# A two-layer graph attention network on one core: layer 0's scores in four quarters of TensorE

## The chip, the core and the metric

The kernel runs on one core of one Trainium2 chip. The core has five engines that work side by side and wait for one another through semaphores: TensorE (matrix products out of SBUF into PSUM), VectorE, ScalarE, GpSimd, and SyncE, which here only issues transfers. The metric is the time of one execution on the device in microseconds; the figure quoted is the median of three runs.

## The reference

The input is x, 8 batches of 2048 nodes with 256 features, and one adjacency matrix of 2048 x 2048. Two graph layers follow, each with a residual sum and a layer norm. Layer 0 is an attention with 4 heads of 64 features, in which the softmax is taken separately in each chunk of 256 keys and the results of the 8 chunks are summed:

```python
scores = jnp.einsum('bhnd,bhjcd->bhnjc', q, kc) / jnp.sqrt(jnp.asarray(Dh, dtype=q.dtype))
scores = jnp.clip(scores, -10.0, 10.0)
mask = adj_matrix.reshape(N, Nc, CHUNK)[None, None]
scores = jnp.where(mask == 0, jnp.asarray(-10.0, scores.dtype), scores)
attn = jax.nn.softmax(scores, axis=-1)
ctx = jnp.einsum('bhnjc,bhjcd->bhnd', attn, vc)
```

Then come an output projection, a residual, a norm with scale and shift, and another residual with a norm. Layer 1 is a graph attention whose score is a sum of a source and a target term, with a leaky slope of 0.2, a mask, a softmax over all 2048 nodes, the product with the transformed features, and an ELU. All arithmetic is f32.

## The kernel before

**Tiles.** A tile has P = 128 partitions. Queries are taken CH = 512 at a time (NCH = 4 groups), heads in pairs (HP = 2), keys in chunks of 256 (NK = 8), that is KT = 2 tiles of 128 keys. One combination of a query group, a pair of heads and a chunk is a *slot*, so a batch has SLOTS = 4 x 2 x 8 = 64 slots. `qT` and `kT` hold queries and keys transposed: the partitions are the 128 features of a pair of heads (D = 64 for each head), the free axis is the nodes.

**What a slot does for layer 0.**
- `scores(s)` (line 378): for each of the two key tiles `u` it takes two PSUM banks (`ps`, one bank for each head of the pair) and issues one matmul for each head `k`. The weights (`lhsT`) are the 64 feature rows of that head for 128 keys, the moving operand is 512 queries. Head 0 lies on rows 0 to 63 of the array and head 1 on rows 64 to 127, so each matmul uses one half of the rows and all the columns (line 388).
- Line 399, on VectorE: the scores are clipped and masked out of PSUM into `pr` in SBUF, with `slab`, an 8-bit tile of upper bounds.
- `exps` (line 411), on ScalarE: the exponential of `pr`, in place.
- `product(s, k)` (line 425): for each head the probabilities are the weights, 64 queries at a time (`z` chooses a column half of the array), and the values with a column of ones are the moving operand, 65 columns. They use all 128 rows. ScalarE copies the result out (line 432), VectorE takes a reciprocal (line 440), GpSimd scales and adds (lines 447 and 449).

**PSUM.** `two_banks` (line 105) hands out two buffers of two banks in turn. So the scores of one slot fill both buffers, and the next slot's scores wait until VectorE has read them.

**Layer 1.** While layer 0 of batch b runs, layer 1 of batch b - 1 is carried along: in each slot `lower.step()` makes and uses four tiles (STEP = 4): one VectorE instruction makes `e` (line 739), and 16 matmul calls use it as weights in 64-column halves (line 761, into `pa`).

**Order.** The order on every engine is written out by hand: the kernel runs under a manual schedule, and instructions go to an engine in the order in which the code calls them. In a slot `s` of the main loop the order of TensorE's work is the scores of slot s + 1, the product of head 0 of slot s, the layer 1 step, the product of head 1 of slot s, and in some slots a projection, an output product or a transposition. In batch 0 there is no layer 1 step; masks are prepared there instead (`masks.step()`). After batch 7, layer 1 of the last batch runs alone.

Of the kernel before, what the change touches and what calls it, by code (L numbers as in the profile page):

```python
# [17 lines left out]
P = 128  # L18
# [4 lines left out]
def adj_resnorm_kernel(  # L23
# [19 lines left out]
    nc = tc.nc  # L43
    B, N, F = x.shape
    H, D = a_src.shape
# [59 lines left out]
    def two_banks(shape, name):  # L105

        turn_of[0] ^= 1
        return psA.tile(shape, F32, tag=f"psA{turn_of[0]}", name=name)
# [10 lines left out]
    qT = big.tile([P, KC, N], F32, tag="qT", name="qT")  # L119
    kT = big.tile([P, KC, N], F32, tag="kT", name="kT")  # L120
# [257 lines left out]
    def scores(s):  # L378
        q, hp, c = where[s]
        slab = slab_of.pop(s)  # L380
        cols = slice(q * CH, (q + 1) * CH)
        pss = []
        for u in range(KT):
            t = KT * c + u
            ps = two_banks([P, 2, CH], "ps")
            for k in range(2):
                rows = slice(k * D, (k + 1) * D)
                nc.tensor.matmul(  # L388
                    ps[:, k, :],
                    lhsT=kT[rows, hp, t * P : (t + 1) * P],  # L390
                    rhs=qT[rows, hp, cols],
                    start=True,
                    stop=True,
                )
            pss.append(ps)
        probs[s] = []
        for u in range(KT):
            pr = prp.tile([P, 2, CH], F32, tag="pr", name="pr")
            nc.vector.scalar_tensor_tensor(  # L399
                pr,  # L400
                pss[u],
                -CLIP,
                slab[:, u, :].unsqueeze(1).to_broadcast([P, 2, CH]),
                op0=ALU.max,
                op1=ALU.min,
            )
            probs[s].append(pr)
# [548 lines left out]
    for b in range(B):  # L956
        waug = blocks.tile([P, NT, H, D1], F32, tag="waug", name="waug")
        sd = small.tile([P, 2 * H, NT], F32, tag="sd", name="sd", bufs=1)
        if b == 0:
            for s in range(3):  # L960
                load_slab(s)
            scores(0)
            for u in range(KT):
                exps(0, u)
# [7 lines left out]
        for s in range(SLOTS):  # L972
            q, hp, c = where[s]
# [27 lines left out]
            if s + 1 < SLOTS:  # L1001
                scores(s + 1)
# [67 lines left out]
        if b + 1 < B:  # L1070
            (k0, v0, q0), (l1, t1, k1, v1, q1), (l2, t2, k2, v2, q2), (l3, t3, k3, v3, q3) = turns
            rest = [lambda: lower.rest(1)] if lower else []
            order = [begin, *rest, l1, *rest, lambda: before.values((2, 3))]
            order += [*rest, ctx, *rest, *rest, k0]
            order += [steps[0], t1, steps[1], v0, steps[2], steps[3], l2, k1, steps[4], q0]
            order += [steps[5], v1, t2, l3, steps[6], q1, steps[7], k2, steps[8], steps[9], t3, v2]
            order += [lambda: [load_slab(s) for s in range(3)], fs[0], q2, fs[1], k3, fs[2], v3]
            order += [lambda: scores(0), q3, lambda: [exps(0, u) for u in range(KT)]]
        else:

            step = lower.step
            order = [begin, lambda: before.values((2, 3)), steps[0], step, ctx, step, steps[1], step]
            order += [steps[2], step, steps[3], step, steps[4], step, steps[5], step, steps[6], step]
            order += [steps[7], step, steps[8], step, steps[9], step, fs[0], step, fs[1], step, fs[2]]
            order += [step] * 5
            assert sum(p is step for p in order) == LATE
# [64 lines left out]
```

## Time and profile before

| | |
|---|---|
| median of 3 runs | 3769.13 us (3766.95 to 3769.89) |
| the profiled execution: span from first to last instruction | 3764.9 us |
| instructions in the profile | 159631 |
| TensorE: matmul, weight loads | 3655.7 us, 2743.7 us busy |
| VectorE | 3138.5 us busy |
| ScalarE | 1979.9 us busy |
| GpSimd | 1368.3 us busy |
| runs of scores (line 388) | from 60.5 to 3490.9 us |
| mean granted TensorE clock | 0.993 |

Engines overlap, so the busy times don't add up to the span. Weight loads run beside matmuls and have a row of their own. Matmuls are pipelined and their ends are modelled, so the starts of successive records say more of the rate than their durations do. A matmul's shape is written as rows * columns of the array that hold weights, followed by the operand: `64*128 64x512` has 64 rows, 128 columns and 512 moving columns. Each f32 matmul call of the code appears as two matmul records, each with a weight load of its own: the 2048 calls of line 388 are 4096 records. The chain of waits is followed back from the last instruction to whatever released it each time. Idle time of an engine that isn't in this chain costs nothing.

### The profile page before, as it was taken

To read this page: it belongs to the slowest core of one execution; us is meant where nothing else is said; L and a number is where in the kernel's file an instruction comes from. 1 tells how busy PE (TensorE), PEld (TensorE's weight loads), DVE (VectorE), ACT (ScalarE), POOL (GpSimd) and SP (SyncE) were. 2 spreads that over 40 slices of the span, in tenths; PEclk is the share of its full clock that TensorE was granted. 3 is DMA by queue.
4 is the path that set the end of the run, shared out by engine and by line. 5 is a ranking of instruction groups with operands and counts; after the bars stand their busy time and mean duration, and the time that the engine had idled before them with its cause. 6 is when DMAs were issued, how large, how long until landed. Compare 5 with 4: busy or idle time off the path is not lost.

```text
span 3764.9 us, 159631 instructions
## 1 busy us (share of the span) xinstructions
PE 3655.7 (97%) x72100; PEld 2743.7 (73%) x72100; DVE 3138.5 (83%) x4213; ACT 1979.9 (53%) x3571; POOL 1368.3 (36%) x1202
## 2 busy tenths in 40 slices
PE   9999999999999999999999999999999999999787
PEld 5656677776777777776777767777677777776676
DVE  5877589976999689995999959998699977997899
ACT  4666455555555555554555545555555555555322
POOL 1445234333433343333443324433343333334300
PEclk9999999999999999999999999999999999999899
DMA  6653334333333343333433334333433333332344
GB/s 164 152 117 70 80 96 109 105 75 112 109 105 105 86 123 100 104 96 89 133 99 94 101 93 133 106 104 76 113 109 105 105 82 115 111 98 73 100 150 137
DMA packets 672092, 398.46 MB, mean 106 GB/s; under 512 B 427312, under 2 KB 591536, under 8 KB 671408
## 3 DMA queue, kind: packets, MB, share of 16 engines
q1 hardware_dynamic: 621408, 354.55, 35.8%
q10 hardware_dynamic: 50000, 33.70, 2.8%
q8 instruction: 564, 9.24, 1.0%
q14 instruction: 120, 0.98, 0.1%
HBM read 331.22 MB, written 56.89 MB: 103 GB/s over the span
## 4 chain that ended last, share of the span: by engine, by line
PE 84%; DVE 7%; issue 4%; ACT 3%; DMA 1%; SPq 0%; ACTq 0%; POOL 0%; DVEq 0%; POOLq 0%
PE pc L425 25%; PE ps L388 23%; PE pa L761 21%; PE pp L332 5%; PE pw L581 3%; PE po L540 3%; DVE e L739 3%; PE pv L348 2%; DVE pr L399 2%; ACT y L505 1%; ACT pr L411 1%; DVE y L560 0%; DMA xp<-in_x_dram 0%; DVE y L557 0%; ACT qT L340 0%
## 5 line engine op out<-in xcount | busy, mean ns | idle before, releaser
L399 DVE SCALAR_TENSOR_TENSOR pr<-ps,slab 128x1024 f32<-128x1024 f32 x1024 | 1193.7, 1207 | 216.4 <-PE ps L388 212.6
L425 PEld LDWEIGHTS pc<-vaug,pr 128*64 128x64 f32 x32768 | 1038.7, 138 | 404.8 <-issue 298.4
L739 DVE SCALAR_TENSOR_TENSOR e<-srow,gd,et 128x1024 f32<-128x1024 f32 x1024 | 1277.4, 1291 | 14.8 <-PE pa L761 7.6
L425 PE MATMUL pc<-vaug,pr 128*64 128x65 f32 x32768 | 1153.6, 224 | 15.1 <-ACT pr L411 9.6
L761 PE MATMUL pa<-waug,e 128*64 128x65 f32 x32768 | 1070.1, 224 | 45.6 <-DVE e L739 41.4
L761 PEld LDWEIGHTS pa<-waug,e 128*64 128x64 f32 x32768 | 1016.4, 139 | 64.0 <-DVE e L739 55.5
L411 ACT ACTIVATE pr<-pr 128x1024 f32<-128x1024 f32 x1024 | 1040.3, 1055 | 39.7 <-DVE pr L399 30.8
L388 PE MATMUL ps<-qT,kT 64*128 64x512 f32 x4096 | 1024.7, 617 | 3.6 <-DVE pr L399 2.9
L432 ACT COPY raw<-pc 128x260 f32<-128x260 f32 x1024 | 381.3, 373 | 1203.1 <-PE pc L425 1176.4
L447 POOL TENSOR_TENSOR part<-raw,rd 128x512 f32<-128x512 f32 x448 | 468.6, 1046 | 1384.5 <-DVE rd L440 1370.1
L449 POOL TENSOR_TENSOR acc<-acc,part 128x512 f32<-128x512 f32 x448 | 575.3, 1284 | 35.2
L388 PEld LDWEIGHTS ps<-qT,kT 64*128 64x128 f32 x4096 | 347.8, 186 | 321.8 <-issue 201.4
L440 DVE RECIPROCAL rd<-raw 128x8 f32<-128x8 f32 x512 | 100.8, 197 | 120.0 <-ACT raw L432 118.8
L447 POOL TENSOR_TENSOR acc<-raw,rd 128x512 f32<-128x512 f32 x64 | 66.9, 1045 | 343.5 <-DVE rd L440 343.5
L793 ACT ACTIVATE sums<-sums,dn 128x64 f32<-128x64 f32 x504 | 131.9, 337 | 12.2 <-DVE dn L787 12.2
L500 POOL TENSOR_TENSOR rs_c<-rs_c,nhalf 128x4 f32<-128x4 f32 x32 | 52.7, 1647 | 232.5 <-DVE off_c L499 232.5
L581 PE MATMUL pw<-w_sb,x1T 128*128 128x264 f32 x512 | 128.0, 398 | 4.7 <-DVE x1T L294 4.7
L540 PE MATMUL po<-wo_sb,qT 128*128 128x256 f32 x512 | 126.2, 391 | 5.7 <-DVE qT L467 2.8
L332 PE MATMUL pp<-xT,wk_sb 128*128 128x512 f32 x256 | 119.2, 609 | 7.9 <-ACT qT L340 6.6
L332 PE MATMUL pp<-xT,wq_sb 128*128 128x512 f32 x256 | 116.2, 596 | 0.0
L348 PE MATMUL pv<-wv_sb,xT 128*128 128x256 f32 x512 | 115.9, 379 | 0.0
L581 PEld LDWEIGHTS pw<-w_sb,x1T 128*128 128x128 f32 x512 | 95.0, 192 | 25.0 <-DVE x1T L294 4.9
(103 smaller groups left out, 1843.7 us busy)
## 6 DMA issues: line engine op xcount, KB each, us to landing
et<-edgeD SPq DMA_DIRECT2D x512, 256.0 KB, 3.0
slab<-clipD SPq DMA_DIRECT2D x512, 128.0 KB, 3.1
srow<-rowD SPq DMA_DIRECT2D x64, 512.0 KB, 5.1
xg<-in_x_dram SPq DMA_DIRECT2D x32, 512.0 KB, 4.9
x1D<-y ACTq DMA_DIRECT2D x32, 512.0 KB, 3.9
x1g<-x1D SPq DMA_DIRECT2D x32, 512.0 KB, 5.1
out_dram<-o SPq DMA_DIRECT2D x30, 512.0 KB, 3.4
ctxD<-acc ACTq DMA_DIRECT2D x56, 256.0 KB, 2.6
```

The lines of the kernel that those rows point to most:

```text
L332: nc.tensor.matmul(pps[c], lhsT=w[:, kc, c * P : (c + 1) * P], rhs=st["xT"][:, kc, :], start=(kc == 0), stop=(kc == KC - 1),)
L388: nc.tensor.matmul(ps[:, k, :], lhsT=kT[rows, hp, t * P : (t + 1) * P], rhs=qT[rows, hp, cols], start=True, stop=True,)
L399: nc.vector.scalar_tensor_tensor(pr, pss[u], -CLIP, slab[:, u, :].unsqueeze(1).to_broadcast([P, 2, CH]), op0=ALU.max, op1=ALU.min,)
L411: nc.scalar.activation(pr, pr, AF.Exp, scale=0.125)
L425: nc.tensor.matmul(pc[z * D : (z + 1) * D, i, :], lhsT=probs[s][u][:, k, i * P + z * D : i * P + (z + 1) * D], rhs=vaug[:, KT * c + u, 2 * ...
L432: nc.scalar.copy(raws[s][:, k], pc)
L447: nc.gpsimd.tensor_mul(part, raw[:, :, :, :D], rd.to_broadcast([P, 2, QT, D]))
L449: nc.gpsimd.tensor_add(accv, accv, part)
L540: nc.tensor.matmul(po[:, k, :], lhsT=qT[:, c, t * P : (t + 1) * P], rhs=wo_sb[:, c, :], start=(c == 0), stop=(c == KC - 1),)
L581: nc.tensor.matmul(pw[:, k, : F + 2 * H], lhsT=self.x1T[:, c, u * P : (u + 1) * P], rhs=w1_sb[:, c, :], start=(c == 0), stop=(c == KC - 1),)
L739: nc.vector.scalar_tensor_tensor(e[:, :w], self.rows[n][:, :w], self.gd[:, h, j : j + 1], self.edge[k // JG][:, j % JG, :w], op0=ALU.max, ...
L761: nc.tensor.matmul(self.pa[i // QT][z * D : (z + 1) * D, i % QT, :], lhsT=e[:, i * P + z * D : i * P + (z + 1) * D], rhs=self.waug[:, j, h ...
```

## The change

Only the two nested loops around the score matmuls change. Each head's matmul with 128 keys as weights becomes two with 64 keys each. The output of keys `z * 64` to `z * 64 + 63` goes to the same partitions of `ps` as before[...]. So a tile of scores is now computed by four matmul calls, each on a quarter of the array (64 rows, 64 columns), in the order key half 0 of head 0, key half 0 of head 1, key half 1 of head 0, key half 1 of head 1. Queries, PSUM buffers, banks, and everything that reads `ps` stay as they were.

```diff
             ps = two_banks([P, 2, CH], "ps")
-            for k in range(2):
-                rows = slice(k * D, (k + 1) * D)
-                nc.tensor.matmul(
-                    ps[:, k, :],
-                    lhsT=kT[rows, hp, t * P : (t + 1) * P],
-                    rhs=qT[rows, hp, cols],
-                    start=True,
-                    stop=True,
-                )
+            for z in range(2):
+                for k in range(2):
+                    rows = slice(k * D, (k + 1) * D)
+                    nc.tensor.matmul(
+                        ps[z * D : (z + 1) * D, k, :],
+                        lhsT=kT[rows, hp, t * P + z * D : t * P + (z + 1) * D],
+                        rhs=qT[rows, hp, cols],
+                        start=True,
+                        stop=True,
+                    )
             pss.append(ps)
```

## The prediction

> **What bounds the kernel now.** I read the page first: busy shares, then the chain of work that ended last, then the groups of line 388, the line that the change edits.
>
> ```profile
> PE 3655.7 (97%) x72100; PEld 2743.7 (73%) x72100; DVE 3138.5 (83%) x4213; ACT 1979.9 (53%) x3571; POOL 1368.3 (36%) x1202
> ...
> PE pc L425 25%; PE ps L388 23%; PE pa L761 21%; PE pp L332 5%; PE pw L581 3%; PE po L540 3%; DVE e L739 3%; PE pv L348 2%; DVE pr L399 2%; ACT y L505 1%; ACT pr L411 1%; DVE y L560 0%; DMA xp<-in_x_dram 0%; DVE y L557 0%; ACT qT L340 0%
> ...
> L388 PE MATMUL ps<-qT,kT 64*128 64x512 f32 x4096 | 1024.7, 617 | 3.6 <-DVE pr L399 2.9
> ...
> L388 PEld LDWEIGHTS ps<-qT,kT 64*128 64x128 f32 x4096 | 347.8, 186 | 321.8 <-issue 201.4
> ```
>
> TensorE carries 84% of the chain, and the scores alone 23%. Then the chain in order of time, in a stretch where layer 0 of one batch and layer 1 of the batch before run together:
>
> ```profile
> 1499.11 1.08 PE pc L425 x32
> 1500.19 1.87 PE pa L761 x64
> 1502.06 0.93 PE pc L425 x32
> 1502.99 1.92 PE ps L388 x8
> 1504.91 1.08 PE pc L425 x32
> ```
>
> The reader is to see a loop of four TensorE pieces with nothing between them: 1.92 + 1.08 + 1.87 + 0.93 = 5.80 us per slot. There are 64 slots in each of 8 batches, 512 in all, and a slot has one such run of scores: 8 matmul records, 1.92 us. From the starts of these runs, some 51 of the 63 intervals of each batch after the first are shorter than 5.83 us, and most are 5.80; the longer ones hold the projections. Batch 0 has no layer 1 beside it, and its chain (60 to 270 us) has TensorE for little over half; I count TensorE as the bound for half of it. In the later batches VectorE, the next engine, has room on average:
>
> ```profile
> 880.00:1310.00 430.00, 427.73 (x8912) 325.22 (x8911) 380.22 (x504) 236.38 (x427) 166.81 (x146) 1.00 0.39 106
> ```
>
> The columns after the length are TensorE, its weight loads, VectorE, ScalarE and GpSimd: VectorE is busy for 380 of 430 us, 88%. A slot could lose up to some 0.6 us before VectorE sets the pace.
>
> Now the run of scores itself, by the instructions of its tile in narrow windows (a matmul's line, then that of the first product after it):
>
> ```profile
> L388 PEld LDWEIGHTS ps<-qT,kT x2: 183/183/183, 1502.9 to 1502.9; 64*128 64x128 f32 x2
> L388 PE MATMUL ps<-qT,kT x2: 693/693/693, 1502.9 to 1502.9; 64*128 64x512 f32 x2
> ```
>
> ```profile
> L425 PE MATMUL pc<-vaug,pr x2: 271/271/271, 1504.8 to 1504.8; 128*64 128x65 f32 x2
> ```
>
> ```profile
> 1502.92 1.99 PE L388 MATMUL ps<-qT,kT 64*128 64x512 f32 x8
> ...
> 1504.84 0.28 PE L425 MATMUL pc<-vaug,pr 128*64 128x65 f32 x2
> ```
>
> Each f32 matmul of the code is two records (2048 calls, 4096 records). The two that start together must be the two row halves[...]. So the run is four rounds of two records. The first pair takes 693 ns and later ones 589: 104 ns in which the first weights are loaded and nothing streams. The run's 1.99 us are 0.104 + three steps + 0.589, which gives 0.43 us a step; the starts of the records put it at 429 ns, and the two of a pair 7 ns apart. A record's end is modelled 0.16 us beyond its step (589 - 429), so the last stream ends near 1504.75, and the first load of the products starts at 1504.84: about 91 ns[...]. Sum: 104 + 4 x 429 + 7 + 91 = 1918 ns, the chain's 1.92.
>
> [...]91 to 96 ns between the last stream and the first load at each change between scores and products, none between lines 425 and 761 (both 128x64), and pairs 7 ns apart. [...]The trace of before shows pairs from two halves, which at least needs something to pass the blocked second pass of the first half; how far that reaches is not shown.
>
> **The change, part by part.** 2048 calls of 64 rows x 128 columns x 512 become 4096 of 64 x 64 x 512: per slot, 8 matmul records and 8 loads become 16 and 16. Nothing on VectorE, ScalarE, GpSimd or a DMA queue moves; the instruction stream grows by 8192 records beside 144200, and that fetch is 1.0% of the DMA engines' time now. The PSUM waits stay where they are: one before a tile's first load, one signal after its last matmul.
>
> (a) Streaming. The array's cells are as full as before: two halves of 64 x 128, or four quarters of 64 x 64. If four run at once, a tile's scores are still two rounds of 429 ns and a slot's are four. No gain and no loss. That two column tiles can stream at once at nearly full rate is shown by line 761: 64 records in 1.87 us, 58 ns for a pair of 65 columns, 0.90 ns a column; a score column costs 429/512 = 0.84 ns. Bounds: 429 if the difference is a fixed few ns per record, 0.90 x 512 = 459 if it is a rate. I take 430, as a small fixed part explains a 65-column stream best.
>
> (b) The first weight load. With 64 columns instead of 128 it should cost what it costs the products after the same kind of change of mode: 271 - 222 = 49 ns (222 is the usual product, 224 the mean on the page). Against 104 that is 55 ns less per slot. The other bound is no gain, if only two quarters load at a time (2 x 49 = 98). I take 49: the two products also load two column tiles at once over all 128 rows, as much data at a time as four quarters. The second tile's loads lie behind streaming, before and after.
>
> (c) Stagger. The fourth quarter starts 3 x 7 = 21 ns after the first, where the second half started at 7: 14 ns more.
>
> (d) Drain. 64x64 is still another mode than 128x64, so both drains stay, about 92 ns each. The trace has no change of mode without one. Bounds: zero change, or -184 ns if equal column widths should spare it; I take none.
>
> Sum per slot: 49 + 4 x 430 + 21 + 91 = 1881 against 1918, -37 ns. Batches 1 to 7: 448 slots x 37 = 16.6 us, of which I keep 95% for slots where TensorE waits anyway, 15.7. Batch 0: 64 x 37 x one half = 1.2. Together 17 us: the span 3764.9 becomes 3748, and the median of the runs, 3769.1 (4.2 us around the span), becomes 3752. The next limit, VectorE, isn't touched by 0.6% of a slot.
>
> **The rivals.**
> 1. The quarters don't overlap fully[...]. To start the fourth quarter at once, TensorE must pass the blocked second passes of three others: its first pass is the 13th and 14th instruction of the tile, where now the second half's is the 5th and 6th. If the third and fourth quarter start only with the second pass of the first two, each tile still chains into the next (second pass of the last quarters beside the first pass of the next tile's first), so a slot has five rounds instead of four: 49 + 5 x 430 + 21 + 91 = 2311, +393 ns. 448 x 0.393 = 176, batch 0 half of 64 x 0.393 = 13: +189 us, 3958. [...]For it: no row of before needs more than about 5.[...] This is the case on the other side.
> 2. The quarters go in turn, two at a time, with no chaining: eight rounds, 49 + 8 x 430 + 112 = 3601, +1683 ns; 448 x 1.683 = 754 and most of batch 0, 86: +840, 4609. For it: no row shows more than two at once. Against: nothing in the array is used twice by the four.
> 3. Four streams are a little slower: 442 to 459 ns a round. At 442: 4 x 12 more than 430, so +11 ns a slot, +5 us, 3774; at 459, +79 ns, +37 us, 3807. Loads two at a time (98 instead of 49) give +12 ns, near +6 us. These end around no change.
> 4. The drain goes: -37 - 184 = -221 ns a slot, about -100 us, 3670. Against: every change of mode in the trace has it.
>
> **How the numbers follow.** Forecast 58%, rival 1 20%, rival 2 10%, rival 3 9% (half within the bound, half above), rival 4 3%. A measurement of this kernel tells 0.2%, about 7.5 us, from no change. Faster: the forecast less 3% in which over half of the 17 us is lost, plus rival 4, so 0.58. Same: those 3% and rival 3's lower half, 0.08. Slower: the rest, 0.34. The predicted time is that of the forecast, 3752, with its own range 3740 to 3762. As cases of both signs matter, the range goes on to the first rival and takes its bounds in: 3740 to 3970, leaving out rivals 2 and 4 and a few per cent of the edges.
>
> **What would show it.** In the changed kernel the group of line 388 has 8192 records of 64x64. Right: four records start within about 21 ns, the first with 589 + 49 = 638 ns, four rounds of 429, the run in the chain 1.88 us, the slot 5.76 us. Rival 1: a round more, the run 2.3 us, starts in groups of two or three. Rival 2: 3.6 us. Rival 3: steps above 440 ns or first records near 690. Wrong in kind would be a slot in which VectorE or a PSUM wait ends last instead of line 388, or a gap that is no longer near 92 ns before and after the run.

## The result and the profile after

The changed kernel takes 3759.34 us (median of 6 runs, 3754.80 to 3761.21) against 3769.51 us before (6 runs). The ratio is 0.9971, 95% interval 0.9960 to 0.9983: 10 us faster, between 6 and 15. Run twice more, the same program took 3755.49 us (ratio 0.9964, 0.9951 to 0.9976) and 3757.51 us (0.9967, 0.9955 to 0.9980). The profiled execution's span went from 3764.9 to 3757.5 us. Lines below the edit move down by one, so the scores are now line 389.

On the page of the changed kernel, the busy engines, the chain by line, and the groups of the scores:

```profile
PE 3640.8 (97%) x76196; PEld 2654.5 (71%) x76196; DVE 3141.6 (84%) x4213; ACT 1981.8 (53%) x3571; POOL 1368.3 (36%) x1202
...
PE pc L426 24%; PE ps L389 22%; PE pa L762 21%; PE pp L332 5%; PE po L541 3%; PE pw L582 3%; DVE pr L400 2%; DVE e L740 2%; PE pv L348 2%; ACT y L506 1%; ACT pr L412 1%; SPq L282 1%; DMA xp<-in_x_dram 0%; DVE y L561 0%; ACT edge L253 0%
...
L389 PE MATMUL ps<-qT,kT 64*64 64x512 f32 x8192 | 1005.6, 604 | 4.8 <-DVE pr L400 3.2
...
L389 PEld LDWEIGHTS ps<-qT,kT 64*64 64x64 f32 x8192 | 256.7, 132 | 366.2 <-issue 229.8
```

Twice the records, and yet the group's busy time fell by 19 us (1024.7 to 1005.6). So four quarters do run at once: in the profile of before the scores' records started in pairs. The chain in order of time, in the same kind of stretch as before:

```profile
1501.97 1.88 PE ps L389 x16
1503.85 1.08 PE pc L426 x32
1504.93 1.87 PE pa L762 x64
1506.80 0.93 PE pc L426 x32
```

The scores take 1.88 us instead of 1.92, the slot 5.76 instead of 5.80; the other three pieces are unchanged to the hundredth. The instructions that start in the first 50 ns of that run, its weight loads and its matmuls:

```profile
L389 PEld LDWEIGHTS ps<-qT,kT x4: 129/129/129, 1501.9 to 1501.9; 64*64 64x64 f32 x4
L389 PE MATMUL ps<-qT,kT x4: 640/640/640, 1501.9 to 1501.9; 64*64 64x512 f32 x4
```

Four matmuls start together, and they last 640 ns where the first pair of before took 693: the exposed load is 640 - 589 = 51 ns instead of 104. Over all 511 runs of scores the median from the first load to the first load of what follows is 1877 ns (1918 before); later rounds are still 429 ns apart, and the gaps between streams and loads before and after the run are still 96 and 91 ns.

Where, then, is the rest? I compared the intervals between the starts of successive runs of scores with the same intervals of the profile of before. In batches 1 to 7 most of them (405 of 446) are 40 ns shorter, within 2 ns; all 446 would give 18 us. Batches 1 to 7 gained 12.8 us (3051.5 to 3038.7). The difference sits in a few places. Two slots of each batch (slot 1 and slot 61) gain nothing or lose 40 ns, 0.8 us in all. And 14 intervals are 0.1 to 1.1 us longer than that change gives, 6.0 us in all; the profile of before has one such pause, of 0.35 us, in a slot where the changed kernel has none. On the other side, slots 52 and 53 of batch 7 gained 1.5 us that the quarters didn't bring: the trace of before has TensorE's granted clock at half from 3437.4 to 3440.8 us, that of the changed kernel has it at full speed in these slots. The longest of the 14, in the timeline of the changed kernel:

```profile
2277.18 0.45 PE L426 MATMUL pc<-vaug,pr 128*64 128x65 f32 x6
...
2278.44 0.97 PE L426 MATMUL pc<-vaug,pr 128*64 128x65 f32 x25 [0.82 <-issue]
```

After six matmuls of a product that needs no new data between its instructions, TensorE idles for 0.82 us, and no engine or transfer released it ("issue"). The DMA view from 2266 to 2279 us, the busy share in 40 slices of tenths, then by queue:

```profile
DMA  0032999940048997997872689976322000049788
...
q1 hardware_dynamic: 2025, 2.33, 56.8%
q8 instruction: 2, 0.03, 1.3%
```

The instruction queue, q8, brings TensorE's program in packets of 16 KB, 256 instructions (596 packets against 564 before: 32 more, for 8192 more instructions). In batches 1 to 7 a packet comes 5.3 us after the one ahead in the median, half of them 4.6 to 6.3 us after; here one was at 2266.93 and the next at 2276.02, after a long burst of data. So theory F for the experiments: TensorE sometimes runs out of instructions, because a packet comes late behind bursts of transfers. Its rivals: that the missing part is chance (theory C in the expectations), or chance and slots that something else paces (theory V).

### The profile page after: what moved, and what is told of

The parts are those of the page before. It is cut to its first block, busy times and chain, and to the rows that moved or that the text cites. A ratio compares the mean times of both kernels' runs of the same rounds, so it can differ in the third digit from the quotient of the medians.

```text
span 3757.5 us, 167823 instructions
## 1 busy us (share of the span) xinstructions
PE 3640.8 (97%) x76196; PEld 2654.5 (71%) x76196; DVE 3141.6 (84%) x4213; ACT 1981.8 (53%) x3571; POOL 1368.3 (36%) x1202
## 4 chain that ended last, share of the span: by engine, by line
PE 81%; DVE 8%; issue 4%; ACT 4%; DMA 2%; SPq 1%; POOL 0%; ACTq 0%; DVEq 0%; POOLq 0%
PE pc L426 24%; PE ps L389 22%; PE pa L762 21%; PE pp L332 5%; PE po L541 3%; PE pw L582 3%; DVE pr L400 2%; DVE e L740 2%; PE pv L348 2%; ACT y L506 1%; ACT pr L412 1%; SPq L282 1%; DMA xp<-in_x_dram 0%; DVE y L561 0%; ACT edge L253 0%
## 5 line engine op out<-in xcount | busy, mean ns | idle before, releaser
L426 PE MATMUL pc<-vaug,pr 128*64 128x65 f32 x32768 | 1155.2, 224 | 17.6 <-ACT pr L412 10.2
L389 PE MATMUL ps<-qT,kT 64*64 64x512 f32 x8192 | 1005.6, 604 | 4.8 <-DVE pr L400 3.2
L389 PEld LDWEIGHTS ps<-qT,kT 64*64 64x64 f32 x8192 | 256.7, 132 | 366.2 <-issue 229.8
L294 DVE STREAM_TRANSPOSE xT<-xp 128x1024 f32<-128x1024 f32 x28 | 34.8, 1244 | 96.6 <-PE pw L582 57.9
```

The costliest lines, as they stand in the source:

```text
L389: nc.tensor.matmul(ps[z * D : (z + 1) * D, k, :], lhsT=kT[rows, hp, t * P + z * D : t * P + (z + 1) * D], rhs=qT[rows, hp, cols], start=Tr ...
L426: nc.tensor.matmul(pc[z * D : (z + 1) * D, i, :], lhsT=probs[s][u][:, k, i * P + z * D : i * P + (z + 1) * D], rhs=vaug[:, KT * c + u, 2 * ...
```

## The experiments

All intervals were treated as above; each is named by the slot whose scores begin it. "Stalls" are intervals in batches 1 to 7 that are over 0.1 us longer than the same interval of before with the kernel's usual change, without slots 1 and 61 and without slots 52 and 53, where in batch 7 the clock differs. "At a packet" are those of them in which TensorE had to wait for its instructions, as told below the table. "End" is what follows the start of the last run of scores but one.

| kernel | median us | span us | batch 0 | batches 1-7 | end | stalls | at a packet |
|---|---|---|---|---|---|---|---|
| before | 3769.51 | 3764.9 | 372.6 | 3051.5 | 280.4 | - | - |
| changed | 3759.34 | 3757.5 | 374.9 | 3038.7 | 283.5 | 14, 5.95 us | 12, 4.85 us |
| changed, second run | 3755.49 | 3753.9 | 371.9 | 3038.0 | 283.6 | 10, 5.33 | 9, 5.03 |
| changed, third run | 3757.51 | 3755.6 | 372.6 | 3038.9 | 282.6 | 15, 6.15 | 14, 5.83 |
| split | 3774.16 | 3773.4 | 374.3 | 3057.1 | 281.7 | 6, 1.68 | 6, 1.68 |
| before, few mask loads | 3767.76 | 3764.4 | 372.7 | 3051.3 | 280.1 | 0 | 0 |
| changed, few mask loads | 3753.19 | 3751.4 | 374.9 | 3035.6 | 280.2 | 6, 2.93 | 3, 1.58 |
| changed, no residual load | 3753.97 | 3752.2 | 374.5 | 3036.7 | 280.6 | 8, 3.85 | 6, 1.84 |
| eight tiles | 3764.15 | 3764.3 | 372.4 | 3048.8 | 282.6 | 22, 13.52 | 19, 12.83 |
| loads in halves | 3755.69 | 3752.7 | 375.1 | 3035.8 | 280.7 | 3, 2.23 | 1, 0.68 |
| loads in halves, small masks | 3754.13 | 3751.2 | 373.0 | 3034.7 | 283.2 | 4, 1.34 | 0 |

The traces test theory F directly. With TensorE's instructions (its semaphore waits among them) sorted by their starts, every 256th is the first of a new packet: of the 23 pauses of over 120 ns between two starts inside a product or a layer 1 step in the changed kernel's batches 1 to 7, 9 end at the same place in the count of 256, and none of the 15 pauses of before share a place. In the median over these batches a packet's first instruction starts 3.7 us after the packet has landed, and nowhere in the trace sooner than 1.28 us. In 12 of the 14 stalls it starts 1.28 to 1.44 us after, the least that the trace shows, so I take it that TensorE had nothing left to run when the packet came; the last column counts stalls in which that time is under 1.6 us. The others are something else, most of them the change from one batch to the next (slot 63) or slot 49 of batch 7, which is 0.2 to 0.3 us longer in every kernel of the table with quarters or eight tiles.

**The changed kernel again, twice.** No edit.

> The changed kernel once more, for a second profile. The change took 40 ns from nearly every slot, which would be 18 us over batches 1 to 7, and the span shows 7.4 us less. Theory F: some slots stall because TensorE's instructions arrive late (256 at a time, behind bursts of data transfers); then stalls of 0.1 to 1 us inside runs of scores or products come again, at other places, some 3 to 6 us in all, and the time is 3755 to 3762. Theory V: the missing part is chance in batch 0 and slots at the batches' ends that something else paces; then the stalls inside batches 1 to 7 don't come again, and this profile's batches 1 to 7 gain 16 us or more.

> The changed kernel a third time, beside the two above: 3754 to 3760, with stalls at slots 5 to 9, 33 and 49 once more, 5 to 6 us in all over what the slots alone give (theory F), or elsewhere and of another size (theory C).

The stalls came again, of the same total, and largely at the same slots: 5 and 6, 33, 49 (the first expectation had them at other places). These follow the 512 KB loads of `x1g` (issued in slots 0, 3 and 7) and `xg` (slots 16, 32, 48). Other transfers are issued there too: `x1t` loads in slots 33 and 49, and a third load of 512 KB, `srow`, just ahead of the stalls in slots 5, 13, 28 and 36. Batches 1 to 7 gained 13.4 and 12.6 us, not 16. That speaks against chance. Batch 0 differs by 3 us from profile to profile of the same program: 374.9, 371.9 and 372.6 us, with TensorE's granted clock at half for 10.2, 3.4 and 6.8 us of it (before: 372.6 and 3.4). A part of the gap between the three medians (3755.5 to 3759.3) can be that.

**As many instructions, without quarters ("split").**

```diff
+            for w in range(2):
             for k in range(2):
...
-                    ps[:, k, :],
+                        ps[:, k, w * 256 : (w + 1) * 256],
...
-                    rhs=qT[rows, hp, cols],
+                        rhs=qT[rows, hp, q * CH + w * 256 : q * CH + (w + 1) * 256],
```

> The kernel before with each score matmul cut into two of 256 queries: two row halves as before, but as many TensorE instructions as the changed kernel. Per slot: first load exposed as before, eight rounds of 216 instead of four of 429 ns, so +12 ns, +5 us over 448 slots. Theory F adds late instructions as in the changed kernel, +3 to +6 us: 3777 to 3781. Theory V: 3773 to 3775, with no more stalls than before.

The price per slot was right (5.81 us). Stalls were 1.7 us, all at a packet: more than before, less than the 3 to 6 that theory F said. The time, 3774.16 us, is the one that theory V gave (3773 to 3775). So theory F missed the size here: the instruction count alone does not set the stalls, and why this kernel has fewer of them than the changed one, with as many instructions, isn't shown. What the run does show is that the gain comes from the quarters and not from more or finer instructions.

**Fewer mask loads, before and after.** Layer 1 keeps its first four mask tiles in each batch.

```diff
+                if k > AHEAD_E:
+                    self.edge[k] = self.edge[k - AHEAD_E - 1]
+                    return
                 et = edges.tile([P, JG, WIDE * P], U8, tag="et", name="et")
```

> The kernel before, where layer 1 loads only its first four mask tiles in each batch and uses them again (the mask of later nodes is not applied): 508 of 540 loads of 256 KB are gone, the rest of the program is the same. It gives the base for the next run. Theory F: few late instructions, 0 to 6 us less than before. Theory V: no change but for batch 0's chance, within 4 us.

> The changed kernel with the same loads left out (layer 1's mask of later nodes is not applied). Theory F: with the bursts gone instructions arrive in time, so the quarters give their full 40 ns a slot against the run of the kernel before with these loads left out: 16 to 20 us less, and stalls under 1 us in batches 1 to 7. Theory V: the difference stays near 10 us.

(480 of 512 loads are gone, counted from the page; the expectation's figures were wrong.) The kernel before doesn't care: 0.9998, interval 0.9990 to 1.0007. The changed kernel's stalls halve to 2.9 us, of which 1.6 us at a packet, all in slots 5 and 6, and batches 1 to 7 gain 15.7 us over their own base (3051.3 to 3035.6; 1.5 of it again by the clock in slots 52 and 53). By the medians the quarters are worth 14.6 us here. Less than the 16 to 20 of theory F, which had also said under 1 us of stalls; above the 10 of its rival.

**No residual load in layer 1's closing.**

```diff
-            self.x = blocks.tile([P, QT, F], F32, tag="xb", name="x1g")
-            nc.sync.dma_start(out=self.x, in_=by_node(x1D, b, g))
+            self.x = self.h
```

> The changed kernel, where layer 1's closing doesn't load its residual (x1g, 512 KB four times a batch) and adds its own input in its place, so that the last residual sum is not the network's. Theory F (instructions arrive late behind bursts of transfers): the stalls at slots 5, 6, 7 and 9 of batches 2 to 7, which follow these loads and make 2.2 to 3.1 us in the two profiles of the changed kernel, are gone; those at slots 33 and 49, which follow another load of 512 KB (xg), stay. Time 2 to 4 us under the changed kernel: 3752 to 3756. Theory C (the stalls are chance): as many stalls as before, at slots 5 to 9 too, 3755 to 3760.

The test by place. Stalls at slots 5 to 9 fell from 3.1, 2.2 and 2.1 us in the three profiles of the changed kernel to 0.4 us; those at slots 33 and 49 made 1.3 us, against 1.4, 3.2 and 3.4. So the stalls behind the loads that were left out went, as said; that the others stayed as they were holds against the first profile only.

**Eight tiles.**

```diff
-            for z in range(2):
+            for z in range(4):
...
-                        ps[z * D : (z + 1) * D, k, :],
+                        ps[z * 32 : (z + 1) * 32, k, :],
```

> Eight tiles of 64 rows and 32 columns instead of four quarters: 32 score matmul records per slot and as many loads. If passing blocked instructions reaches as far as some 26 instructions, a slot takes a first load of about 25 ns, four rounds of 429, a stagger of 7 x 7 = 49 and the drain of 91: 1881 ns, about the changed kernel's 1877, so the slots give the same gain and the time is 3756 to 3766 with the stalls of late instructions grown (theory F: 64 instructions per slot instead of 32). If the reach is shorter, a round or more is added: +0.43 us per slot, over 3930.

A dose of instructions: 64 for the scores of a slot. The first lines of a run of scores, by tile:

```profile
L389 PEld LDWEIGHTS ps<-qT,kT x12: 103/103/106, 1506.6 to 1506.6; 64*32 64x32 f32 x12
L389 PE MATMUL ps<-qT,kT x8: 613/613/613, 1506.6 to 1506.6; 64*32 64x512 f32 x8
```

Eight matmuls start within 46 ns, with an exposed load of 613 - 589 = 24 ns, and the run takes 1878 ns: the shorter load saves 27 ns against the quarters, and the stagger takes 26 ns more. So the slots gain as much as with quarters, but the stalls grow to 13.5 us, at the same kind of slots, and the time is 3764.15 us (0.9986, 0.9980 to 0.9993). 48 added instructions per slot instead of 16, and over twice the stalls, 12.8 us of them at a packet. With the packets' own times and the two tests on loads, theory F is shown for these stalls. What sets their number isn't: "split" has as many instructions as the changed kernel and fewer stalls.

**Quarters for one tile, halves for the other ("mixed").** The first key tile of a slot keeps the quarters, the second goes back to the loop of before.

> Quarters for the first key tile of a slot, two row halves for the second. If every change of tiling mode empties the array and exposes the next first load[...], a slot pays one change more: 49 + 2 x 429 + 21 + 92 + 104 + 2 x 429 + 7 + 91 = 2080 ns against 1918, +162 ns, +73 us in batches 1 to 7 and a few us in batch 0: 3840 to 3850. If only a change to or from the products' mode costs it, the second tile's load hides behind the first tile's streaming and the time is that of the changed kernel, 3752 to 3760.

3841.15 us, as the first theory said. The chain and the first instructions of the second tile:

```profile
1502.85 1.02 PE ps L390 x8
1503.87 1.06 PE ps L400 x4
```

```profile
L390 PE MATMUL ps<-qT,kT x4: 589/589/589, 1503.3 to 1503.3; 64*64 64x512 f32 x4
L400 PEld LDWEIGHTS ps<-qT,kT x2: 183/183/183, 1503.8 to 1503.8; 64*128 64x128 f32 x2
L400 PE MATMUL ps<-qT,kT x2: 693/693/693, 1503.8 to 1503.8; 64*128 64x512 f32 x2
```

The two tiles take 2.08 us together. The first load of line 400, at 1503.80, comes only after the last streams of line 390, which start at 1503.3 and take 429 ns: of the 1.02 us between the first loads of the two lines, 51 + 2 x 429 + 20 leave 91 ns, the same gap as after a run of the changed kernel. Its matmuls have 693 ns again. So here a change of shape from 64x64 to 64x128 cost that gap and an exposed load of 104 ns.

**A version with short bursts.** The `x1g` and `xg` loads go in two halves, in successive slots; the bias that needs the second half is one slot later. Then also the mask tiles one at a time.

```diff
+        nc.sync.dma_start(out=dst[:, :2, :], in_=src[:, :2, :])
+        outgoing.append(lambda: nc.sync.dma_start(out=dst[:, 2:, :], in_=src[:, 2:, :]))
...
-    JG = 2
-    AHEAD_E = 3
+    JG = 1
+    AHEAD_E = 7
```

> The changed kernel with the two 512 KB loads (x1g and xg) each issued as two loads of 256 KB in successive slots, and the addition that needs the second (bias) one slot later. Nothing is left out. Theory F: the bursts are half as long, the stalls at slots 5 to 9, 33 and 49 shrink from 5 us to under 2, and the time is 3751 to 3755. Theory C: no change from the changed kernel, 3755 to 3760.

> The kernel with the 512 KB loads in halves, and layer 1's mask tiles loaded one at a time (128 KB, seven ahead) instead of two at a time (256 KB, three ahead). Nothing is left out. Theory F: the bursts are shorter still, late instructions are as rare as in the run without mask loads, batches 1 to 7 gain 15 to 17 us, and the time is 3750 to 3754. Theory C: as the changed kernel in the same comparison.

The stalls shrink to 2.2 and 1.3 us, and those at a packet to 0.7 and none (the rest is something else than late instructions); batches 1 to 7 gain 15.7 and 16.8 us. The medians, 3755.69 (0.9966, 0.9954 to 0.9979) and 3754.13 us (0.9961, 0.9949 to 0.9974), beat the kernel before, but lie just above what theory F expected (to 3755 and to 3754) and can't be told from the changed kernel (3755.5 to 3759.3): the intervals overlap, and batch 0 and the end vary by as much as there is to gain.

**The end of batch 7 ("tail").** After the scores the changed kernel's three profiles show an end that is 2.2 to 3.2 us longer than before. Among the first profile's waits, with total, times and longest:

```profile
PE pt L474 <- POOL acc L450: 2.4, 2, 1.8
```

In the profile of before TensorE never waits for this accumulation of GpSimd's. The edit, on top of the version with small loads, moves the multiplication ahead of it to VectorE for the last slots:

```diff
-        nc.gpsimd.tensor_mul(part, raw[:, :, :, :D], rd.to_broadcast([P, 2, QT, D]))
+        mul.tensor_mul(part, raw[:, :, :, :D], rd.to_broadcast([P, 2, QT, D]))
```

> As the kernel with small loads, and in the last batch's last 18 slots the product with the reciprocal (line 448) on VectorE instead of GpSimd. If GpSimd's last accumulation is what TensorE waits for before the last context (1.8 us in the changed kernel), the wait goes and the time is 1 to 2 us under the kernel with small loads: 3748 to 3753. If something else is late there by as much, it is the same.

A miss: 3763.41 us. The wait at the context is down to 0.3 us, but now GpSimd waits for VectorE; the waits between 3440 and 3560 us:

```profile
POOL acc L454 <- DVE part L452: 34.0, 8, 9.4
```

The multiplication came up to 9.4 us after GpSimd was ready for it. Most of the loss is ahead of the end: batches 1 to 7 take 3041.6 us against 3034.7 without this edit. What makes the end longer isn't known. The wait for GpSimd doesn't go with it: it is 1.5 us in the run without the residual load, where the end is as short as before (280.6 us), and 0.6 us with small loads, where the end takes 283.2. Late instructions don't go with it either: in the ends of the changed kernel's first and third profile no packet's first instruction starts within 1.6 us of landing.

## Why the prediction was right, step by step

- **Direction and mechanism** were right, and 3759 us lies in the likeliest case's own range (3740 to 3762); the gain was 10 us (11 to 13 in the repeats) where 17 were forecast. In the profiles, 1.5 us of the gain were luck: slots 52 and 53 of batch 7, where that of before shows half the clock.
- **(a) Streaming** at 430 ns a round: measured 429. The doubt of 459 ns, from the rate of the 65-column products, fell; "eight" shows 429 per 512 columns too, "split" 216 per 256.
- **(b) First load** of 49 ns: measured 51, all four at once.
- **(c) Stagger** of 21 ns: measured 20 (rounds start at 1, 8, 15 and 21 ns).
- **(d) Drain**, the gap at a change of mode, that is, of the shape of the weights: measured 96 and 91 ns, unchanged; "mixed" shows 91 ns between two kinds of score tiles as well. Not every change of shape has the gap: in the profile of before a weight load of line 655 (128x4) starts at 421.71 us, 1 ns after the last matmul of line 348 (128x128), beside its stream. The sum of 1881 ns came out as 1877.
- **The batch-0 term**, -1.2 us, was within what two profiles of one program differ by: the changed kernel's three gave +2.4, -0.7 and 0.0, so it is neither shown nor refuted.
- **The mis-sized term** is the factor of 95% for slots that gain nothing (0.8 us by the prediction), together with the sentence that costed the longer instruction stream at nothing, as 1.0% of the DMA engines' time. Slots 1 and 61 cost 0.8 us, as allowed for; the late instructions cost 4.9 to 5.8 us on top. A share of bandwidth was the wrong measure: in 12 of the 14 stalls the packet's first instruction started within 1.44 us of landing, where the median is 3.7. The end took back 2.2 to 3.2 us more, for a reason that stays open.
- **Rivals 1 and 2** (the fourth quarter can't start at once) fell: the 13th and 14th instruction of a tile start within 20 ns of the first two, ahead of the second passes of three other calls, and with eight tiles the 29th and 30th do within 46 ns. That it would reach so far, and the 20% for rival 1, was my estimate: the profile of before shows pairs, 7 ns apart, and no more. Rival 3 fell with (a), rival 4 with (d).

One slip in the part on the kernel: a slot makes two layer 1 tiles (STEP = 128 / 64 = 2), not four; the 64 records of line 761 in a slot belong to two tiles. No sum of the prediction used it.

## What to carry to other kernels

In these profiles the first weight load of a run of scores was on the path, and its exposed part went with the columns of a tile (104, 51 and 24 ns for 128, 64 and 32 columns): cutting tiles to 64 columns saved 53 ns a run, paid back in part by 13 ns of stagger. The streaming gained nothing here (429 ns a round in both kernels), so look for such gains only where a run is short or a change frequent, and keep the same shape through a run: with one change inside it, "mixed" takes 2.08 us where the kernel before takes 1.92. The 8192 added instructions had to be fetched too, in 32 more packets: before counting on 1%, see whether the instruction packets land in time during the largest transfers. Cutting those transfers into shorter ones brought the stalls from 5.3 to 6.2 us down to 2.2 and 1.3 us here, though what it saved was too little for the medians to show.

## What the runs showed of the hardware

- TensorE started matmuls of later calls ahead of the second passes of earlier ones. The first passes of four quarters start within 20 ns, and those of eight tiles within 46 ns; the second passes follow 429 ns later. That a call's second pass stands ahead of the next call's first in the instruction stream, a stall of the changed kernel shows: the packet whose first instruction starts at 918.50 us (1.37 us after landing) begins inside a run's second tile. Of the three passes of that tile that came ahead of it, two start at 917.93 and 917.94 us, and the third, where other tiles have the next quarter's first pass 7 ns later, at 918.36, 429 ns after the first. Within 12 ns of the new packet's first load three more matmuls start; the last two follow at 918.98 and 918.99.
- Eight tiles of 64x32 stream 512 f32 columns in the same 429 ns as two of 64x128.
- In the changed kernel TensorE stood still for 0.1 to over 1 us where a 16 KB packet came late, mostly 7 to 9 us after the last one. After landing, a packet's first instruction never started sooner than 1.28 us there, and 1.37 us in the profile of before. Weight loads and matmuls make 288 instructions per slot of 5.76 us (16 and 16 of the scores, 64 and 64 of the products, 64 and 64 of layer 1), more than the 256 of a packet.
- In the profile of before the granted clock is at half from 3437.4 to 3440.8 us, and a run of scores there is 2.96 us long where the one 9 us later is 1.99. The changed kernel has no such stretch in batches 1 to 7, and its two slots there took 1.5 us less.
